# A graph layer on one core: the opening's transfers rearranged, and the one-hot of an edge step put back beside its selection

## The chip, the core and the metric

The kernel runs on one core of one Trainium2 chip. The metric is device time in microseconds (us), the median of three runs. The engines are named as the profile names them: PE (TensorE: matmuls; PEld is its weight loads), DVE (VectorE), ACT (ScalarE), POOL (GpSimd), SP (SyncE, which here only issues DMAs). "SPq", "ACTq" and so on are the engines' instruction queues, which issue DMAs.

## The reference

A graph has N = 12,500 nodes with 160 features each (64 scalars and 32 vectors of 3) and E = 400,000 edges, sorted by destination. What is computed, cut to what matters:

```python
h_s = s @ lin1_ws * a / sqrt(64)                   # s: 64 scalars of a node, a: its attribute
h_v = einsum('nci,cd->ndi', v, lin1_wv) * a / sqrt(32)
hid = silu(edge_scalars @ fc_w1 / sqrt(64))        # 64 scalars an edge
w1..w5 = split(hid @ fc_w2 / sqrt(64))             # 224 weights an edge
es, ev = h_s[edge_src], h_v[edge_src]              # gather
m_s = concat(w1*es*e0, w4 * sum_i(ev*e1) / sqrt(3))
m_v = concat((w2*es) x e1, w3*ev*e0, w5*cross(ev, e1) / sqrt(2))
agg = segment_sum(m, edge_dst) / sqrt(16)
pre = sc(s, v) * a + agg @ lin2 * a                # sc: another linear map of the node itself
x   = layernorm(x + gate(pre))                     # silu of 64 scalars, sigmoid gates of the vectors
```

## The kernel before

**Opening.** All nodes go through the first linear map. The nodes are taken 2048 at a time (`CH`), six full groups and one of 212. For each group SP's queue loads two halves of `xa` (64 scalars on partitions 0 to 63, two of the three vector components on 64 to 127, four DMAs of 64 x 1024 values) and `xz` (the third component, in four quarters of 512 nodes one under the other, four DMAs of 32 x 512), lines 269 to 281. PE multiplies by `l1` and by the block-diagonal `l1z`, DVE scales by the node's attribute into `ht`, and ACT's queue stores `ht` as rows of 640 B into the table `h_tab` in device memory (L345). Ahead of the node loads SP's queue issues three strided loads of `rows`, the first destination of each block of three tiles, 1042 values of 4 B taken one by one from `dst` (L254, L255). The function `bases` (L292) turns `rows` into a base for each block on all partitions (`lo`). After the node loads SP's queue loads the first edge indices and attributes (`index(0)`), the first chunk of edge scalars (`load_chunk(0)`), and the weights, `fc_w2` in ten pieces with its columns in another order. ACT's queue loads all destinations `dt` (L351) behind the stores of `h`; DVE subtracts the bases from them (`rel`, L387 and L392). The weights of the second map (`l2`) are loaded by SP (L380) and scaled by DVE one by one (L111). All this stands in an order written out by hand; the queues take it in that order, though the scaling of `l2` is mixed in with the first edge steps. DMAs of SP and ACT share eight completion semaphores in turn, and an issue waits for the DMA that had its semaphore before it.

**Edge steps.** 3125 tiles of 128 edges are taken four at a time: 782 steps. A step n

- gathers four tiles' rows of `h_tab` by the edges' sources: four indirect DMAs on POOL's queue into one of four buffers `hg` (L427);
- makes 224 weights an edge on PE (`pw`, L440) from `hid`, which PE (`ph`, L418) and ACT (L420) made two steps ahead for two steps at once, out of chunks of edge scalars `es` (L228) that SP loads;
- multiplies weights and rows on DVE, four instructions (`pr`, L450 once and L458 three times); the last of them frees the step's `hg` and `pw`;
- makes the selection on DVE: `one_hot` compares `rel` with 0 to 15 (`oh`, L503), and `select_quad` multiplies this by the four edge attributes (`sel`, L512);
- two steps later, multiplies `sel` and `pr` on PE into the sums of a pair of blocks (`pa`, L519).

Closed blocks are copied by ACT (L711), turned by PE (L528), mapped by `l2` sixteen at a time (`po`, L543) and added by DVE, block by block, to the accumulator `acc` at a position that depends on the data (L551, 1042 additions). Nodes whose blocks are done are finished four tiles at a time (L577 to L616) in between.

The order within a step is that of the program (`manual_schedule`). The loop before has the one-hot a step ahead and the additions at the first of the four products' gaps:

```python
oh = one_hot(edge, steps[0][2])
for n, (c, i, tiles) in enumerate(steps):
    ...
    pr = products(edge, pw, hg, len(tiles), [first, lambda: None])   # first: pops 1 or 2 additions
    sel = select_quad(edge, tiles, oh)
    for a in ready:
        add(*a)
    if n + 1 < len(steps):
        oh = one_hot(edge, steps[n + 1][2])
```

`first` pops two additions in even steps and one in odd ones; they are executed behind the selection.

Of the kernel before, what the change touches and what calls it, by code (L numbers as in the profile page):

```python
# [10 lines left out]
F32 = mybir.dt.float32  # L11
# [9 lines left out]
P = 128  # L21
S = 64
V = 32
# [5 lines left out]
BT = 3  # L29
# [3 lines left out]
KB = 4  # L33
SIDE = KB * BT
CT = 2 * SIDE
AHEAD = 3 * CT
# [4 lines left out]
NWT = 224  # L41
# [12 lines left out]
def gnn_kernel(  # L54
# [21 lines left out]
    nc = tc.nc  # L76
    N = x.shape[0]
    NT = attr.shape[1]
# [4 lines left out]
    NB = -(-TT // BT)  # L83
# [3 lines left out]
    consts = ctx.enter_context(tc.tile_pool(name="consts", bufs=1))  # L87
    dram = ctx.enter_context(tc.tile_pool(name="dram", bufs=1, space=bass.MemoryType.DRAM))
    h_tab = dram.tile([N, D], F32, name="h_tab")
# [5 lines left out]
    in_order = ctx.enter_context(ExitStack())  # L95
    in_order.enter_context(tc.manual_schedule(
        engines={ENG.PE, ENG.DVE, ENG.Activation, ENG.Pool, ENG.SP}))
    at = consts.tile([P, NT], F32, name="at")
    nc.scalar.dma_start(at, attr)

    l1 = consts.tile([P, P], F32, name="l1")
    nc.vector.memset(l1, 0.0)
    nc.scalar.dma_start(l1[:S, :S], lin1_ws)
    for i in range(2):
        r = slice(S + i * V, S + (i + 1) * V)
        nc.scalar.dma_start(l1[r, r], lin1_wv)
    scales = [(l1[:S], 1.0 / math.sqrt(S)), (l1[S:], 1.0 / math.sqrt(V))]

    def scale():
        for m, by in scales:  # L110
            nc.vector.tensor_scalar_mul(m, m, by)  # L111
        scales.clear()

    def block_diagonal(name, w, n, scale, queue=nc.scalar):
        k = w.shape[0]
        m = consts.tile([n * k, n * k], F32, name=name)
        nc.vector.memset(m, 0.0)
        for i in range(n):
            queue.dma_start(m[i * k:(i + 1) * k, i * k:(i + 1) * k], w)
        if scale != 1.0:  # L120
            scales.append((m, scale))
        return m

    l1z = block_diagonal("l1z", lin1_wv, 4, 1.0 / math.sqrt(V))
    for m, by in scales:
        nc.scalar.mul(m, m, by)
    scales.clear()


    rel = consts.tile([P, TT], I16, name="rel")  # L130
    rows = consts.tile([1, NB], I32, name="rows")
    early = consts.tile([1, 1], F32, name="early")
# [8 lines left out]
    ends_pool = ends.enter_context(tc.tile_pool(name="ends", bufs=1))  # L141
# [21 lines left out]
    steps = []  # L163
# [3 lines left out]
    slot_of = {}  # L167
# [23 lines left out]
    def index(t):  # L191
        a0, idx, _ = ahead(t)
        return idx[:, t - a0:t - a0 + 1]
# [20 lines left out]
    def in_pairs(a):  # L214

        return a.rearrange("o (c k h) -> o h c k", k=KB, h=2)

    ess = {}

    def load_chunk(c):  # L220
        if c in ess:
            return
        t0, halves = chunks[c]
        es = ess[c] = loads.tile([2 * S, SIDE * P], F32, name="es")
        for half, n in enumerate(halves):
            to = es[half * S:(half + 1) * S]
            e0 = (t0 + half * halves[0]) * P
            nc.sync.dma_start(to[:, :n * P], es_t[:, e0:e0 + n * P])  # L228


    ident = consts.tile([P, P], F32, name="ident")
# [9 lines left out]
    w2 = consts.tile([2 * S, 2, NWT], F32, name="w2")  # L241
# [4 lines left out]
    even = NB // (2 * KB) * 2 * KB  # L246
# [1 line left out]
                   base=0, channel_multiplier=0)  # L248
    nc.gpsimd.iota(share[:, even:], pattern=[[RATE, NB - even]], base=even * RATE, channel_multiplier=0)

    with nc.allow_non_contiguous_dma(reason="the first destination of each block"):
        firsts = dst[0:1, 0:(even - 1) * BT + 1:BT].rearrange("o (c h k) -> o h c k", k=KB, h=2)
        for half in range(2):
            nc.sync.dma_start(in_pairs(rows[:, :even])[:, half], firsts[:, half])  # L254
        nc.sync.dma_start(rows[:, even:], dst[0:1, even * BT:(NB - 1) * BT + 1:BT])  # L255


    U = 4
    dt = ends_pool.tile([P, TT], I32, name="dt")
    lo = ends_pool.tile([P, NB], F32, name="lo")  # L260
    CH = 4 * U * P
    starts = list(range(0, N, CH))
    with tc.tile_pool(name="nodes", bufs=len(starts)) as nodes, tc.tile_pool(
        name="nodes_ps", bufs=6, space=PSUM
    ) as nps, tc.tile_pool(name="z_ps", bufs=2, space=PSUM) as zps:
        loaded = []
        for c0 in starts:
            cn = min(CH, N - c0)
            quarters = 4 if cn == CH else 1
            assert quarters == 4 or cn <= U * P  # L270
            xa = nodes.tile([P, CH], F32, name="xa")
            for b0 in range(0, cn, CH // 2):
                b1 = min(b0 + CH // 2, cn)
                nc.sync.dma_start(xa[:S, b0:b1], xs_t[:, c0 + b0:c0 + b1])
                nc.sync.dma_start(xa[S:, b0:b1], xv_t[:2 * V, c0 + b0:c0 + b1])
            xz = nodes.tile([P, U * P], F32, name="xz")
            cq = cn // quarters
            for q in range(quarters):
                nc.sync.dma_start(xz[q * V:(q + 1) * V, :cq],
                                  xv_t[2 * V:, c0 + q * cq:c0 + (q + 1) * cq])  # L280
            loaded.append((c0, cn, quarters, cq, xa, xz))
        index(0)
        load_chunk(0)
        for half in range(2):
            r = slice(half * S, (half + 1) * S)
            nc.sync.dma_start(w1[r, r], fc_w1)
            at_c = 0
            for a, b in ((64, 128), (0, 64), (192, 224), (160, 192), (128, 160)):
                nc.sync.dma_start(w2[r, half, at_c:at_c + b - a], fc_w2[:, a:b])
                at_c += b - a  # L290

        def bases():  # L292

            base_f = ends_pool.tile([1, NB], F32, name="base_f")
            nc.vector.tensor_copy(base_f, rows)
            for b0 in range(0, NB, U * P):
                b1 = min(NB, b0 + U * P)
                ps = nps.tile([P, U, P], F32, name="hp").rearrange("p u c -> p (u c)")
                nc.tensor.matmul(ps[:, :b1 - b0], ones, base_f[:, b0:b1], start=True, stop=True)
                nc.scalar.copy(lo[:, b0:b1], ps[:, :b1 - b0])  # L300
            nc.vector.tensor_sub(share, rows, share)
            nc.vector.tensor_reduce(early, share, AX.X, OP.min)
            nc.vector.tensor_scalar(early, early, -float(MARGIN), None, op0=OP.is_lt)

        for c0, cn, quarters, cq, xa, xz in loaded:
# [4 lines left out]
            first = c0 // P  # L310
# [14 lines left out]
                                            at[:n, first + full:first + full + 1], None, op0=OP.mult)  # L325

            pz = zps.tile([P, U, 4, V], F32, name="pz")
            k = quarters * V
            for u in range(-(-cq // P)):
                n = min(P, cq - u * P)  # L330
                nc.tensor.matmul(pz[:n, u, :quarters].rearrange("p q c -> p (q c)"),
                                 xz[:k, u * P:u * P + n], l1z[:k, :k], start=True, stop=True)
            if quarters == 4:
                nc.vector.tensor_mul(
                    ht[:, :, P:].rearrange("p (q u) c -> p u q c", q=4), pz,
# [5 lines left out]
            if cn > full * P:  # L341
                n = cn - full * P
                nc.vector.tensor_scalar(ht[:n, full, P:], pz[:n, full, 0],
                                        at[:n, first + full:first + full + 1], None, op0=OP.mult)
            nc.scalar.dma_start(  # L345
                h_tab[c0:c0 + full * P, :].rearrange("(q p) d -> p q d", p=P), ht[:, :full])
            if cn > full * P:
                nc.scalar.dma_start(h_tab[c0 + full * P:c0 + cn, :], ht[:n, full])


    nc.scalar.dma_start(dt, dst)  # L351
    iota = consts.tile([P, W], F32, name="iota")
    nc.vector.tensor_copy(iota, iota_i)
    nc.vector.tensor_scalar_mul(w2, w2, 1.0 / math.sqrt(64))

    scs = consts.tile([S, V3], F32, name="scs")
    nc.sync.dma_start(scs, sc_ws)
# [137 lines left out]
            sorted_eat[a0] = eas  # L495
        return sorted_eat[a0]

    def one_hot(pool, tiles):

        n = len(tiles)  # L500
        t0 = slot_of[tiles[0][0]]
        oh = pool.tile([P, Q, W], F32, name="oh4")[:, :n]
        nc.vector.tensor_tensor(oh, rel[:, t0:t0 + n, None].to_broadcast([P, n, W]),  # L503
                                iota[:, None, :].to_broadcast([P, n, W]), op=OP.is_equal)
        return oh

    def select_quad(pool, tiles, oh):

        n = len(tiles)
        u = slot_of[tiles[0][0]] % AHEAD  # L510
        sel = pool.tile([P, Q, 4, W], F32, name="sel", bufs=3)
        nc.vector.tensor_mul(  # L512
            sel[:, :n], oh[:, :, None, :].to_broadcast([P, n, 4, W]),
            by_slot(tiles[0][0])[:, u:u + n, :, None].to_broadcast([P, n, 4, W]))
        return sel
# [112 lines left out]
    with tc.tile_pool(  # L628
# [132 lines left out]
        def add_up(n):  # L761

            if not adds or adds[0][0] > n:
                return []
            _, b, os, k, base = adds.pop(0)
            waiting.discard(blocks_of(b // 2)[b % 2])
            return [(base, os, k)]
# [15 lines left out]
        with tc.manual_schedule(engines={ENG.PE, ENG.DVE, ENG.Activation, ENG.Pool}):  # L783
# [3 lines left out]
            pieces = list(range(0, N, CHN))  # L787
            products_due = []
            checks = farthest(late)
            oh = one_hot(edge, steps[0][2])  # L790
            for n, (c, i, tiles) in enumerate(steps):
                if 2 <= n < 2 + ZP // 2:
                    for k in range(2):
# [11 lines left out]
                def first(n=n):  # L805
                    if rest:
                        rest()
                    for _ in range(2 - n % 2):
                        ready.extend(add_up(n))

                pr = products(edge, pw, hg, len(tiles), [first, lambda: None])
                sel = select_quad(edge, tiles, oh)
                for a in ready:
                    add(*a)
                if n + 1 < len(steps):
                    oh = one_hot(edge, steps[n + 1][2])
                if step_on:
                    step_on()
                begin()
# [153 lines left out]
```

## Time and profile before

| | |
|---|---|
| median of three runs | 5045.04 us (5044.53 to 5065.4) |
| profiled execution, time | 5044.53 us |
| profiled execution, span | 5042.8 us |
| first gather issued | 78.36 us |
| first product of the edge steps | 92.58 us |
| busy: PE, POOL, DVE, ACT | 78%, 59%, 47%, 18% |
| granted clock of PE, mean | 0.885 |
| mean rate of all DMAs | 82 GB/s |

A busy share is an average over the opening and 782 steps that are alike. Which wait ends last in a step is read from the idle time ahead of an engine's instruction and from what ended it. "remote" is a release that the profile can't put down to an instruction close by.

### The profile page before, as it was taken

Reading aid. Unit: us, or ns where it says so; the run is one execution under the profiler, and the core shown is the slowest. Engines: PE = TensorE matmul, PEld = TensorE weight load, DVE = VectorE, ACT = ScalarE, POOL = GpSimd, SP = SyncE. Lnnn points to the kernel's source line nnn. Section 1 sums busy time; section 2 is a strip of 40 time slices with the busy share of each in tenths; the row PEclk is TensorE's granted clock in tenths of the full one; section 3 lists DMA queues with packets and bytes.
Section 4 is the critical chain, followed back from the end, with each engine's and each line's share of the span. In section 5 each row is a group of like instructions: output and inputs, shape, how many; then the busy total and the mean of one; then the engine's idle time right before and its main releaser. Section 6 shows DMA issues by size and latency. Waiting matters only on the chain. (4 is left out here: it accounts for less than half of the span.)

```text
span 5042.8 us, 47689 instructions
## 1 busy us (share of the span) xinstructions
PE 3954.1 (78%) x14291; PEld 1696.2 (34%) x14291; DVE 2348.6 (47%) x6374; ACT 928.2 (18%) x2463; POOL 2991.5 (59%) x3134
## 2 busy tenths in 40 slices
PE   5777878778778888778878777778777877788877
PEld 3333333333333333333333333333333333333333
DVE  4444444444444544445444444444444544444444
ACT  1211121111111111112112111111111221211212
POOL 3565656665666666655666665656655665566563
PEclk8889988888989898888899888889888888888888
DMA  7333333333333333333333333333333333333332
GB/s 195 75 75 81 83 79 79 84 83 75 81 73 86 81 80 84 88 72 79 87 75 81 81 79 81 82 75 77 81 81 74 82 83 76 80 73 87 74 72 51
DMA packets 241211, 411.77 MB, mean 82 GB/s; under 512 B 74200, under 2 KB 171876, under 8 KB 240820
## 3 DMA queue, kind: packets, MB, share of 16 engines
q0 software_dynamic: 150000, 256.20, 21.5%
q1 hardware_dynamic: 77666, 142.75, 12.0%
q10 hardware_dynamic: 13282, 9.69, 0.7%
q8 instruction: 119, 1.95, 0.2%
q14 instruction: 144, 1.18, 0.1%
HBM read 392.40 MB, written 16.00 MB: 81 GB/s over the span
## 5 line engine op out<-in xcount | busy, mean ns | idle before, releaser
L427 POOL DMA_INDIRECT hg<-h_tab,idx x3125 | 2986.7, 956 | 2007.2 <-DVE pr L458 1035.3
L440 PE MATMUL pw<-w,hid 128*128 128x448 f32 x3126 | 1511.6, 610 | 292.5 <-ACT hid L420 103.3
L450 DVE TENSOR_TENSOR pr<-pw,hg 128x512 f32<-128x512 f32 x782 | 538.0, 688 | 2480.9 <-remote 1156.8
L519 PE MATMUL pa<-pr,sel 128*64 128x416 f32 x6250 | 1374.5, 556 | 57.9 <-issue 48.3
L458 DVE TENSOR_TENSOR pr<-pw,hg 128x384 f32<-128x384 f32 x2346 | 1152.3, 545 | 2.4 <-issue 2.2
L440 PEld LDWEIGHTS pw<-w,hid 128*128 128x128 f32 x3126 | 605.8, 212 | 821.9 <-issue 657.2
L519 PEld LDWEIGHTS pa<-pr,sel 128*64 128x64 f32 x6250 | 405.8, 144 | 964.2 <-issue 866.4
L528 PE MATMUL pt<-ident,sa 128*128 128x128 f32 x2084 | 360.6, 299 | 431.1 <-ACT hid L420 266.3
L711 ACT COPY sa<-pa 128x416 f32<-128x416 f32 x521 | 265.7, 510 | 1748.7 <-remote 626.5
L528 PEld LDWEIGHTS pt<-ident,sa 128*128 128x128 f32 x2084 | 258.5, 151 | 760.1 <-issue 368.3
L418 PE MATMUL ph<-es,w 128*128 128x512 f32 (+1 forms) x784 | 447.2, 653 | 42.3 <-ACT tt L533 13.1
L543 PE MATMUL po<-tt,l 128*96 128x256 f32 (+5 forms) x1496 | 376.0, 402 | 65.7 <-ACT tt L533 38.5
L420 ACT ACTIVATE hid<-ph 128x512 f32<-128x512 f32 x392 | 234.4, 598 | 968.5 <-remote 479.3
L512 DVE TENSOR_TENSOR sel<-oh,eas 128x256 f32<-128x256 f32 x782 | 324.4, 415 | 0.6 <-issue 0.5
L543 PEld LDWEIGHTS po<-tt,l 128*96 128x96 f32 (+1 forms) x1496 | 240.8, 173 | 223.1 <-issue 102.8
L531 ACT COPY tt<-pt 128x192 f32<-128x192 f32 x521 | 165.6, 318 | 772.4 <-remote 206.1
L418 PEld LDWEIGHTS ph<-es,w 128*128 128x128 f32 x784 | 118.4, 190 | 311.3 <-issue 258.5
L551 DVE TENSOR_TENSOR acc<-acc,os 96x32 f32 x1042 | 205.2, 197 | 18.9 <-ACT os L546 7.1
L503 DVE TENSOR_TENSOR oh<-rel,iota 128x64 f32<-128x64 int16 x782 | 170.0, 217 | 0.0
L533 ACT COPY tt<-pt 128x64 f32<-128x64 f32 x521 | 117.2, 225 | 0.0
L420 ACT ACT_TABLE_LOAD x48 | 61.6, 1283 | 248.4 <-remote 187.9
L546 ACT COPY os<-po 96x512 f32<-96x512 f32 (+2 forms) x68 | 38.3, 563 | 312.2 <-PE po L543 118.6
(77 smaller groups left out, 614.9 us busy)
## 6 DMA issues: line engine op xcount, KB each, us to landing
es<-in_es_t_dram SPq DMA_DIRECT2D x260, 384.0 KB
hg<-h_tab,idx POOLq DMA_INDIRECT x3125
h_tab<-ht ACTq DMA_DIRECT2D x6, 1280.0 KB
xt<-in_x_dram SPq DMA_DIRECT2D x23, 320.0 KB
out_dram<-y SPq DMA_DIRECT2D x23, 320.0 KB
xv<-in_xv_t_dram SPq DMA_DIRECT2D x25, 187.5 KB
xs<-in_xs_t_dram SPq DMA_DIRECT2D x25, 125.0 KB
xa<-in_xs_t_dram SPq DMA_DIRECT2D x12, 256.0 KB
```

Source lines behind the costliest of these rows:

```text
L418: nc.tensor.matmul(ph[:k, c], w1[:k, :k], es[:k, t0 * P + c0 * P:t0 * P + c1 * P], start=True, stop=True)
L420: nc.scalar.activation(hid[:k, c], ph[:k, c], AF.Silu, scale=1.0 / math.sqrt(64))
L427: nc.gpsimd.indirect_dma_start(out=hg[:, t, :], out_offset=None, in_=h_tab, in_offset=bass.IndirectOffsetOnAxis(ap=i, axis=0))
L440: nc.tensor.matmul(pw[:, t:t + m, :NWT], hid[:m * S, c * P:(c + 1) * P], w2[:m * S, :m], start=True, stop=True)
L450: nc.vector.tensor_mul(two, pw[:, :n, :2 * S].rearrange("p t (k c) -> p t k c", k=2), hg[:, :n, None, :S].to_broadcast([P, n, 2, S]))
L458: nc.vector.tensor_mul(pr[:, :n, first:first + V3].rearrange("p t (i c) -> p t i c", i=3), pw[:, :n, None, 2 * S + k * V:2 * S + (k + 1) * ...
L512: nc.vector.tensor_mul(sel[:, :n], oh[:, :, None, :].to_broadcast([P, n, 4, W]), by_slot(tiles[0][0])[:, u:u + n, :, None].to_broadcast([P ...
L519: nc.tensor.matmul(pa[half * ROWS:(half + 1) * ROWS, :NPR], sel[:, t].rearrange("p k w -> p (k w)"), pr, start=start, stop=stop)
L528: nc.tensor.transpose(pt[:, four * P:four * P + k], sa[:k, c:c + P], ident[:k, :k])
L543: nc.tensor.matmul(po[:, k, :nb], l2[r, terms[to, part, four]], a[:, :nb], start=(n == 0), stop=(n == len(of) - 1))
L551: nc.vector.tensor_add(window, window, os[:, :, b])
L711: nc.scalar.copy(sa, pas.pop(j)[:, :NPR])
```

## The change

- The loads of a node group are three DMAs instead of eight: 64 x 2048, 64 x 2048, and for `xz` one DMA of 128 rows, which now stand with the quarter as the fast index of the partition; `l1z` is laid out to match.
- The first group's loads are the first of SP's queue; the weights of the first map (ACT's queue) and the other groups follow.
- The strided loads of `rows` are gone. One row of `dst` (3125 values) is loaded to partition 0 on ACT's queue, and DVE copies the bases out of it at the start of `bases`, in three instructions.
- The stores of `h` (the full rows of tiles), the first chunk of edge scalars and all of `dt` go on POOL's queue, ahead of the gathers. The last 84 rows are stored on SP's queue.
- `fc_w2` is loaded in one piece for each half, and DVE orders and scales it in ten instructions instead of one.
- In a step, the one-hot is made just ahead of its selection, in `select_quad`; the additions are popped one in each of two gaps, so up to two in every step.

In the built program the scalings of `l2` now all stand ahead of the first product on DVE, and SP's loads of `l2` behind the store of the last 84 rows.

```diff
-    with nc.allow_non_contiguous_dma(reason="the first destination of each block"):
-        firsts = dst[0:1, 0:(even - 1) * BT + 1:BT].rearrange("o (c h k) -> o h c k", k=KB, h=2)
-        for half in range(2):
-            nc.sync.dma_start(in_pairs(rows[:, :even])[:, half], firsts[:, half])
-        nc.sync.dma_start(rows[:, even:], dst[0:1, even * BT:(NB - 1) * BT + 1:BT])
...
+        def load(c0):
...
-            for b0 in range(0, cn, CH // 2):
-                b1 = min(b0 + CH // 2, cn)
-                nc.sync.dma_start(xa[:S, b0:b1], xs_t[:, c0 + b0:c0 + b1])
-                nc.sync.dma_start(xa[S:, b0:b1], xv_t[:2 * V, c0 + b0:c0 + b1])
+            nc.sync.dma_start(xa[:S, :cn], xs_t[:, c0:c0 + cn])
+            nc.sync.dma_start(xa[S:, :cn], xv_t[:2 * V, c0:c0 + cn])
             xz = nodes.tile([P, U * P], F32, name="xz")
             cq = cn // quarters
-            for q in range(quarters):
-                nc.sync.dma_start(xz[q * V:(q + 1) * V, :cq],
-                                  xv_t[2 * V:, c0 + q * cq:c0 + (q + 1) * cq])
+            z = xv_t[2 * V:, c0:c0 + cq]
+            if quarters == 4:
+                nc.sync.dma_start(xz[:, :cq], bass.AP(tensor=z.tensor, offset=z.offset,
+                                                      ap=[[z.ap[0][0], V], [cq, 4], [1, cq]]))
+            else:
+                nc.sync.dma_start(xz[S:S + V, :cq], z)
             loaded.append((c0, cn, quarters, cq, xa, xz))
+
+        load(starts[0])
...
+        nc.scalar.dma_start(dt[0:1], dst[0:1])
+        for c0 in starts[1:]:
+            load(c0)
         index(0)
-        load_chunk(0)
+        raw = ends_pool.tile([2 * S, NWT], F32, name="raw")
...
         def bases():
 
+            firsts = dt[0:1, 0:(even - 1) * BT + 1:BT].rearrange("o (c h k) -> o h c k", k=KB, h=2)
+            for half in range(2):
+                nc.vector.tensor_copy(in_pairs(rows[:, :even])[:, half], firsts[:, half])
+            nc.vector.tensor_copy(rows[:, even:], dt[0:1, even * BT:(NB - 1) * BT + 1:BT])
...
-            nc.scalar.dma_start(
+            nc.gpsimd.dma_start(
                 h_tab[c0:c0 + full * P, :].rearrange("(q p) d -> p q d", p=P), ht[:, :full])
             if cn > full * P:
-                nc.scalar.dma_start(h_tab[c0 + full * P:c0 + cn, :], ht[:n, full])
-
-
-    nc.scalar.dma_start(dt, dst)
+                nc.sync.dma_start(h_tab[c0 + full * P:c0 + cn, :], ht[:n, full])
+
+
+    load_chunk(0, nc.gpsimd)
+    nc.gpsimd.dma_start(dt, dst)
...
-    def one_hot(pool, tiles):
+    def select_quad(pool, tiles):
...
-                    for _ in range(2 - n % 2):
-                        ready.extend(add_up(n))
-
-                pr = products(edge, pw, hg, len(tiles), [first, lambda: None])
-                sel = select_quad(edge, tiles, oh)
+                    ready.extend(add_up(n))
+
+                pr = products(edge, pw, hg, len(tiles), [first, lambda n=n: ready.extend(add_up(n))])
+                sel = select_quad(edge, tiles)
                 for a in ready:
                     add(*a)
-                if n + 1 < len(steps):
-                    oh = one_hot(edge, steps[n + 1][2])
```

## The prediction

> **What bounds the kernel now.** I read the page's costliest groups first, then the list of waits, and then the timeline of the opening and of a piece in the middle. The groups show who is busy and who waits.
>
> ```profile
> span 5042.8 us, 47689 instructions
> ...
> L427 POOL DMA_INDIRECT hg<-h_tab,idx x3125 | 2986.7, 956 | 2007.2 <-DVE pr L458 1035.3
> ...
> L450 DVE TENSOR_TENSOR pr<-pw,hg 128x512 f32<-128x512 f32 x782 | 538.0, 688 | 2480.9 <-remote 1156.8
> ...
> L458 DVE TENSOR_TENSOR pr<-pw,hg 128x384 f32<-128x384 f32 x2346 | 1152.3, 545 | 2.4 <-issue 2.2
> ...
> L512 DVE TENSOR_TENSOR sel<-oh,eas 128x256 f32<-128x256 f32 x782 | 324.4, 415 | 0.6 <-issue 0.5
> ...
> L503 DVE TENSOR_TENSOR oh<-rel,iota 128x64 f32<-128x64 int16 x782 | 170.0, 217 | 0.0
> ```
>
> GpSimd issues 3125 gathers. From the first at 78.36 us to the end of the last (4998.3 + 0.95) are 4920.9 us, and these are 2986.7 us of issue and 2007.2 - 73.0 us of idle time. VectorE waits 2480.9 us, nearly always ahead of the first product of a step (L450). The waits say for what GpSimd's idle time is:
>
> ```profile
> POOL hg L427 <- DVE pr L458: 1035.3, 262, 10.8
> POOL hg L427 <- issue: 947.6, 2798, 73.0
> ```
>
> 0.30 us between two gathers is the queue's own; 1035.3 us in 262 waits go to the last product of a step, which frees one of four `hg` buffers. Such a wait looks like this in the timeline:
>
> ```profile
> 2523.89 0.69 DVE L450 TENSOR_TENSOR pr<-pw,hg 128x512 f32<-128x512 f32 x1 [10.34 <-remote]
> ...
> 2525.89 0.41 DVE L512 TENSOR_TENSOR sel<-oh,eas 128x256 f32<-128x256 f32 x1
> ...
> 2526.24 0.94 POOL L427 DMA_INDIRECT hg<-h_tab,idx  x1 [5.26 <-DVE pr L458]
> 2526.39 0.21 DVE L503 TENSOR_TENSOR oh<-rel,iota 128x64 f32<-128x64 int16 x1
> ```
>
> VectorE had been idle for 10.34 us; four products then run end to end, and GpSimd goes on 2.35 us after the first of them began. So the time is the opening up to the gathers, plus gathers, plus waits that end with a product's end. The selection (L512), the one-hot (L503) and the additions (L551) stand behind the products.
>
> The opening is the second thing that the change touches:
>
> ```profile
> 0.75 1.99 SPq L254 DMA_DIRECT2D rows<-in_dst_dram  x2
> ...
> 7.22 0.54 SPq L274 DMA_DIRECT2D xa<-in_xs_t_dram  x1
> ...
> 74.93 0.80 ACTq L351 DMA_DIRECT2D dt<-in_dst_dram  x1
> ...
> 78.36 1.13 POOL L427 DMA_INDIRECT hg<-h_tab,idx  x1 [73.00 <-issue]
> ...
> 85.67 6.26 DVE L387 TENSOR_TENSOR rel<-dt,lo 128x260 int16<-128x260 int32 x12
> ...
> 108.05 0.94 POOL L427 DMA_INDIRECT hg<-h_tab,idx  x1 [3.81 <-DVE l L111]
> ```
>
> The strided loads of `rows` hold SP's queue until 7.22 us. Then the DMA engines are the bound:
>
> ```profile
> 20.00:30.00 10.00, 5.78 (x52) 5.58 (x51) 5.09 (x8) 0.00 (x0) 0.00 (x0) 0.90 1.05 290
> ...
> 50.00:60.00 10.00, 6.73 (x59) 6.38 (x57) 5.61 (x9) 0.00 (x0) 0.00 (x0) 1.00 1.07 294
> ...
> 90.00:100.00 10.00, 4.08 (x8) 1.75 (x8) 6.64 (x25) 3.49 (x3) 7.56 (x9) 0.81 0.31 70
> ```
>
> The last three columns are clock, DMA share and GB/s: the 16 engines are full (1.05, 1.07) until `dt` has landed, and not after.
>
> **The opening, worked out.** By the packet records, full 2048-node groups take 1536 packets of 4096 B at 265 ns and 768 of 2048 B at 138 ns: (407 + 106) / 16 = 32.1 us. The stores of h are 12,500 rows of 640 B at 36 ns: 28.1 us. `dt` is 128 x 590 ns / 16 = 4.7 us, the first edge scalars 128 x 419 ns / 16 = 3.4 us. Sum 68.3 us of full engines; between the first node load's issue (7.22) and the subtraction that waits for `dt` (85.67) lie 78.4 us, so 10.1 us are latency and gaps.
>
> In the changed kernel the first node load stands first on SP, where L254 began at 0.75 us. The strided loads are gone; the bases come from one 12.5 KB row on ScalarE's queue and three small copies on one partition of VectorE. The nearest row, the conversion of 1042 values (L295), is 0.68 us, so at most 2 us in all, amid nodes work that waits for DMA: nothing, or 2 us if VectorE were the bound there. With the same 78.4 us `dt` lands at 79.2 (6.5 us earlier). If the gaps shrink, because loads no longer share eight completion semaphores with the stores (SP waited 23.0 us in 3 waits for `h_tab<-ht`), down to 2 us, it is 71. I take 75, the middle: 10.7 us earlier.
>
> Two things follow. First, the weights of the second linear map: before, VectorE scaled each as it came, between the first products (L111, up to 107.69 + 0.36), and the 21st gather waited for that until 108.05. Their loads wait on SP behind 27 issues of about 0.65 us, 18 us, which in the new order begin when the last node group is done, some 20 us before `dt`; so the scalings, now all ahead of the first product, are bare time: 21 x 0.18 = 3.8 us. First product at 75 + 6.7 (L387 and L392) + 3.8 = 85.5, instead of 92.58. Ten scalings of the raw weights replace one of 0.40 us: at 0.2 us each 2 us, ahead of the wait for `dt`, hidden. Second, the gathers: they need the stores landed, 8.1 us (`dt`, scalars) before `dt`, so from about 67 on; sixteen take 16 x 1.25 = 20 us to 87, the first buffer is free at 85.5 + 2.2 = 87.7, and the 17th starts at 88, not 99.45; the 21st at 93, not 108.05. Gains of 11.5 and 15; I take 13 us. What is late next is PE's weights, in the usual rhythm.
>
> **The edge steps.** A step's VectorE work is the same 2.16 us of products, 0.41, 0.21 and the additions. Before, the one-hot of step n stood ahead of its product, now behind. Where VectorE was idle before a product, the product starts as soon as PE lets it, in both. In a burst of m steps after that, the chain to the last product is m products and m-1 times the rest, in both. So the gathers' releases do not move: 0. The selection ends up to 0.21 us later, and PE reads it two steps on (12 us): hidden; without that cover, 782 x 0.21 = 164 us, but in the list of waits PE's weight loads wait for `sel` 13.3 us in all, 12 times. Additions go 2 a step for 8 of 12 steps instead of 1.5 for 11; the 1042 x 0.197 us stay. A step with two in place of one makes the next product up to 0.2 us later if VectorE is the late one; bounds from below and above are 0.2 us for a third of the 262 waits, -17 and +17 us. I take 0.
>
> The profiled execution took 5044.53 us, 1.7 us around its span, 0.5 us under the median of 5045.04. Sum: 5044.5 - 13 + 0 = 5031.5; I say 5032.
>
> **The price that no row shows: stores on GpSimd's queue.** Each of the six stores has 2048 rows. The nearest row is a gather of 128 rows, 0.95 us; ScalarE's queue needed 0.37 us for a store. If the 0.95 us is all fixed, six stores are 6 us, hidden between node groups. If it is all per row, a store is 16 x 0.95 = 15.1 us. I take a third of that, 5 us, since GpSimd is idle until 78 us: 15 + 6 x 5 = 45 us, ahead of the stores' own data, so nothing on the path. Below 8.3 us each it stays hidden (15 + 6 x 8.3 = 65).
>
> The Trainium skill, "DMA: Bandwidth & Descriptors", section "Issuing engines are not separate DMA queues", says that DMAs started on several engines run on the same 16 and that this saves only the issuing time. This is the rule against the change: by it the stores gain nothing from moving, and the opening would keep its 68.3 us and gain only the 6.5 us at the front, 5038. The same page's "Latency and other measured facts" puts the software path's first byte at about 1 us; no row here shows a store on it, and by that figure an estimate is 6 us for six stores, hidden.
>
> **Rivals.** *Stores bound by GpSimd (slower).* The first group was ready 13 us after its load's issue (7.22 to 20.29), so now at about 15. At 15.1 us each the last store is issued at 106; about 3 us for the small store, the scalars and `dt`, and 8.1 us of their data put `dt` at 117, the first product at 127.5, the 21st gather at 135 to 137 against 108: +28, 5072. With a price g it comes at 15 + 6g + 3 + 25 = 43 + 6g, so from g = 10.8 us a store on the kernel is slower than before. For: 0.95 us for 128 rows. Against: a gather also reads its indices. Chance 0.18; further 0.05 for a rhythm that loses over 25 us through later selections.
>
> *Opening and rhythm both better (faster).* Gaps go to 2 us (15 to 17 us in all) and the even additions save up to 17 us of the waits: 5044.5 - 16 - 12 = 5016. For: 262 waits, each ended by VectorE. Against: nearly all of them begin with an idle VectorE. Chance 0.25.
>
> *The change saves only the front.* The engines stay full and the gaps stay 10.1 us: 5044.5 - 6.5 = 5038. Chance 0.12. The forecast has 0.40.
>
> **Numbers.** 0.5% is 25 us, about what a measurement of this kernel can tell from no change. Forecast and front alone fall within it: same 0.52; faster 0.25; slower 0.23. The range goes from the faster case's deeper half (5010) to the GpSimd case's price (5072); the likeliest case's own is 5020 to 5043.
>
> **What would show it.** Right: first node load issued near 1 us, `dt`'s subtraction near 75, first product near 85, 21st gather near 93, and GpSimd's wait for products still about 1035 us. Wrong: stores of over 8 us each on GpSimd's queue; a wait sum that moved by over 25 us, which would say that the selection's place or the additions set the releases; PE waiting for `sel`.

## The result, and the profile after

The changed kernel took 5024.9 us (median of 20 runs, 4984.79 to 5047.46), the kernel before beside it 5051.62 us (20 runs, 5035.62 to 5078.56). The ratio is 0.9939, with a 95% interval of 0.9918 to 0.9959: 0.61% faster, 31 us of the mean of the runs; the medians are 26.7 us apart. The forecast was 5032, in a range from 5010 to 5072. The time lies in the range and in the forecast's own, 5020 to 5043, but on the other side of the 0.5% bound, where 0.25 of the chance had been put; the interval reaches across that bound. As a change, 13 us had been forecast, and about 31 (21 to 41) were measured. The profiled execution took 5013.31 us. Single runs of one kernel lie mostly 10 to 20 us, and up to 40, to either side of their median, so one pair of profiles can't show a term of 13 us in the total. What repeats from profile to profile is what to go by: times in the opening, durations, counts.

The costliest groups of the changed kernel, with busy time, mean of one in ns, idle time before them and its main releaser, as in the prediction:

```profile
span 5011.5 us, 47586 instructions
...
L438 POOL DMA_INDIRECT hg<-h_tab,idx x3125 | 3014.2, 965 | 1897.3 <-DVE oh L515 955.2
...
L461 DVE TENSOR_TENSOR pr<-pw,hg 128x512 f32<-128x512 f32 x782 | 539.1, 689 | 2323.0 <-remote 1189.2
...
L518 DVE TENSOR_TENSOR sel<-oh,eas 128x256 f32<-128x256 f32 x782 | 338.0, 432 | 44.0 <-DVE oh L515 1.4
```

Two things have moved that the prediction held still. The gathers' own time is up from 2986.7 to 3014.2 us, and the waits for a buffer are down from 1035.3 to 955.2. They now carry the name of the one-hot (L515) because it follows the last product at once; it is still the product that frees the buffer: in both profiles a gather that waited begins 0.27 us after the last product's end. The selection (L518) takes 432 ns on average, not 415.

The timeline of the opening; columns are start, time, engine, line, and in brackets the idle time before with what ended it:

```profile
0.76 0.58 SPq L235 DMA_DIRECT2D xa<-in_xs_t_dram  x1
1.39 0.58 SPq L236 DMA_DIRECT2D xa<-in_xv_t_dram  x1
8.45 0.60 SPq L241 DMA_DIRECT2D xz<-in_xv_t_dram  x1
...
17.84 1.39 POOL L350 DMA_DIRECT2D h_tab<-ht  x1 [12.47 <-DVE ht L339]
...
51.20 1.15 POOL L350 DMA_DIRECT2D h_tab<-ht  x1 [3.31 <-DVE ht L339]
...
65.03 1.04 POOL L438 DMA_INDIRECT hg<-h_tab,idx  x1 [9.60 <-DMA h_tab<-ht]
...
68.58 6.36 DVE L398 TENSOR_TENSOR rel<-dt,lo 128x260 int16<-128x260 int32 x12 [14.14 <-DMA dt<-in_dst_dram]
...
75.31 4.18 DVE L261 TENSOR_SCALAR l<-l 32x96 f32<-32x96 f32 x20
...
79.63 0.68 DVE L461 TENSOR_TENSOR pr<-pw,hg 128x512 f32<-128x512 f32 x1
...
92.38 0.94 POOL L438 DMA_INDIRECT hg<-h_tab,idx  x1 [0.30 <-issue]
...
113.42 0.94 POOL L438 DMA_INDIRECT hg<-h_tab,idx  x1 [6.36 <-DVE oh L515]
```

A store takes GpSimd 1.15 to 1.39 us. The first gather waits for the last store to land, and the first wait for a buffer comes only at 113.42: until then no gather waits for `dt` or for the scalings (L261). The first seven gathers, 65.03 to 73.40, take 8.9 us instead of 6.6, beside the subtraction (L398) for the most part. In the windows, clock, DMA share and GB/s are the last three columns:

```profile
30.00:40.00 10.00, 8.78 (x37) 6.69 (x38) 5.45 (x8) 1.25 (x3) 0.38 (x1) 0.66 1.03 364
...
50.00:60.00 10.00, 1.10 (x10) 0.83 (x8) 2.74 (x18) 0.00 (x0) 3.35 (x5) 0.76 1.04 350
```

The engines are as full as before (1.03 and 1.04), but they move 364 and 350 GB/s, not 294 at best.

**Where the 31 us went.** The spans of the two profiles differ by 31.3 us. I take the span apart into what lies outside the gathers, the gathers' own time, the 0.305 us that the queue takes between two (3124 x 0.305 = 952.8) and all idle time beyond that. Before: 121.9 + 2986.7 + 952.8 + 981.4 = 5042.8. After: 109.6 + 3014.2 + 952.8 + 934.9 = 5011.5. So -12.3 for the opening and the tail, +27.5 for gathers that got longer, -46.5 for waits. The forecast had -13 and 0.

### The profile page after: what moved, and what is told of

Same layout as the page of the kernel before. It is cut to its first block, busy times and chain, and to the rows that moved or that the text cites. A ratio compares the mean times of both kernels' runs of the same rounds, so it can differ in the third digit from the quotient of the medians.

```text
span 5011.5 us, 47586 instructions
## 1 busy us (share of the span) xinstructions
PE 3956.4 (79%) x14291; PEld 1685.8 (34%) x14291; DVE 2436.2 (49%) x6386; ACT 926.2 (18%) x2463; POOL 3028.5 (60%) x3144
## 5 line engine op out<-in xcount | busy, mean ns | idle before, releaser
L438 POOL DMA_INDIRECT hg<-h_tab,idx x3125 | 3014.2, 965 | 1897.3 <-DVE oh L515 955.2
L525 PE MATMUL pa<-pr,sel 128*64 128x416 f32 x6250 | 1398.3, 559 | 82.2 <-issue 67.1
L549 PE MATMUL po<-tt,l 128*96 128x256 f32 (+5 forms) x1496 | 358.7, 389 | 41.1 <-ACT tt L539 26.3
L518 DVE TENSOR_TENSOR sel<-oh,eas 128x256 f32<-128x256 f32 x782 | 338.0, 432 | 44.0 <-DVE oh L515 1.4
L557 DVE TENSOR_TENSOR acc<-acc,os 96x32 f32 x1042 | 194.7, 187 | 26.0 <-ACT os L552 6.9
L515 DVE TENSOR_TENSOR oh<-rel,iota 128x64 f32<-128x64 int16 x782 | 169.2, 216 | 0.0
L583 PE MATMUL pp<-ident,acc 96*128 96x96 f32 x196 | 38.1, 281 | 127.0 <-DVE acc L557 57.6
```

Source lines behind the costliest of these rows:

```text
L438: nc.gpsimd.indirect_dma_start(out=hg[:, t, :], out_offset=None, in_=h_tab, in_offset=bass.IndirectOffsetOnAxis(ap=i, axis=0))
L518: nc.vector.tensor_mul(sel[:, :n], oh[:, :, None, :].to_broadcast([P, n, 4, W]), by_slot(tiles[0][0])[:, u:u + n, :, None].to_broadcast([P ...
L525: nc.tensor.matmul(pa[half * ROWS:(half + 1) * ROWS, :NPR], sel[:, t].rearrange("p k w -> p (k w)"), pr, start=start, stop=stop)
L549: nc.tensor.matmul(po[:, k, :nb], l2[r, terms[to, part, four]], a[:, :nb], start=(n == 0), stop=(n == len(of) - 1))
L557: nc.vector.tensor_add(window, window, os[:, :, b])
```

## The experiments

Theory A is the prediction's: the opening gives all, the step order nothing. Rival B: the step order gives the other half. The runs were made on three chips (for the first pair of profiles the chip is not on record), four kernels on each beside the kernel before: its medians are 5107.4 us (first four), 5047.79 (second four) and 4068.19 (last four). Ratios are to the kernel before on the same chip.

| run | opening | one-hot | additions | first gather at | gathers' own time | waits beyond the pace | ratio, interval |
|---|---|---|---|---|---|---|---|
| before, first profile | before | step's end | 2 and 1 | 78.36 | 2986.7 | 981.4 | 1 |
| changed, first profile | changed | at selection | 1 + 1 | 65.03 | 3014.2 | 934.9 | 0.9939, 0.9918 to 0.9959 |
| e1_open | changed | step's end | 2 and 1 | 69.20 | 2991.0 | 1022.6 | 0.9992, 0.9971 to 1.0013 |
| e2_step | before | at selection | 1 + 1 | 77.40 | 3017.7 | 999.2 | 1.002, 0.9996 to 1.0044 |
| e5_again | changed | at selection | 1 + 1 | 68.93 | 3008.2 | 951.5 | 0.9958, 0.9938 to 0.9978 |
| e6_open_again | changed | step's end | 2 and 1 | 69.65 | 2983.9 | 1022.5 | 1.0004, 0.9973 to 1.0034 |
| e9_adds | changed | step's end | 1 + 1 | 69.53 | 2986.8 | 0 | 0.9929, 0.9916 to 0.9943 |
| e10_oh | changed | at selection | 2 and 1 | 67.17 | 3013.4 | 0 | 0.998, 0.997 to 0.9991 |
| e11_step_again | before | at selection | 1 + 1 | 77.73 | 3018.4 | 0 | 1.003, 1.0018 to 1.0041 |

**e1_open: the opening alone.** The loop has the step order of before.

```diff
-                    ready.extend(add_up(n))
-                pr = products(edge, pw, hg, len(tiles), [first, lambda n=n: ready.extend(add_up(n))])
-                sel = select_quad(edge, tiles)
+                    for _ in range(2 - n % 2):
+                        ready.extend(add_up(n))
+                pr = products(edge, pw, hg, len(tiles), [first, lambda: None])
+                sel = select_quad(edge, tiles, oh)
...
+                if n + 1 < len(steps):
+                    oh = one_hot(edge, steps[n + 1][2])
```

> The changed opening with the edge steps of before (one-hot at a step's end, additions two and one). In the profiled pair the 21st gather came 15.7 us earlier (92.38 against 108.05), while the profiled time fell by 31 us. Theory A (the step order is worth 0, as predicted, and the rest of the 31 us is spread from run to run): first gather near 65, 21st gather near 92, ratio to before 0.997 (-13 to -16 us of 5050), GpSimd's wait for the products about 1035 us within the spread. Rival B (the step order gives the other 15 us): the same opening, and the same 0.997; it differs from A in the run with the step order alone. Rival C (the opening gives all): 0.994 here.

The opening is there (first gather 69.20, 21st 95.41), the gain in the total is not: 0.9992. The interval just reaches the 0.997 of theory A; rival C is out.

**e2_step: the step order alone.** The kernel before with the other lines of that diff.

> The opening of before with the edge steps of the changed kernel (one-hot just ahead of its selection, additions one in each of two gaps). Theory A (step order worth 0): first gather at 78, 21st at 108, ratio 1.000 within +-0.003. Rival B (fewer or shorter waits for products): ratio 0.997 or less, GpSimd's wait for products some 15 to 80 us under 1035. Rival C (opening gives all): 1.000.

1.002. Rival B's 0.997 is outside the interval. The gathers took 3017.7 us as in the changed kernel, so their 27 us (26.7 here, against e1_open on the same chip) come from the step order and not from the opening.

**e3_act: stores back on ScalarE's queue.**

```diff
-            nc.gpsimd.dma_start(
+            nc.scalar.dma_start(
                 h_tab[c0:c0 + full * P, :].rearrange("(q p) d -> p q d", p=P), ht[:, :full])
             if cn > full * P:
-                nc.sync.dma_start(h_tab[c0 + full * P:c0 + cn, :], ht[:n, full])
+                nc.scalar.dma_start(h_tab[c0 + full * P:c0 + cn, :], ht[:n, full])
```

> The changed kernel with the stores of h issued by ScalarE's queue again; first edge scalars and all destinations stay on GpSimd's queue, loads and steps as changed. Theory Q (the queue decides how a store is cut: 4480-byte packets at 205.6 ns on GpSimd's queue, 640-byte packets at 35.7 ns on ScalarE's): 12,500 packets of 640 B again, 27.9 us of 16 engines in place of 22.8, first gather about 5 us later than 65 (70), and ratio to before about 0.995. Rival (the queue is indifferent; the stores ran faster because the loads' packets were longer or the loads were done): packets and time of the stores as in the changed kernel, first gather 65. Second rival (a store on ScalarE's queue shares completion semaphores with the loads, so gaps come back too): first gather 72 or later.

By the packet records the stores are 12,500 packets of 640 B at 35.6 ns again, 27.8 us of 16 engines, in place of 4480-byte packets at 205.6 ns, 22.8 us: theory Q holds, the queue decides how a store is cut. The first gather came at 75.24, not 70. The timeline of GpSimd has one reason, and the waits of SP's queue have another (in their lines: us in total, times, longest):

```profile
5.33 1.30 POOL L196 DMA_DIRECT2D es<-in_es_t_dram  x2
29.76 0.56 POOL L357 DMA_DIRECT2D dt<-in_dst_dram  x1 [23.13 <-DVE rows L297]
75.24 1.45 POOL L438 DMA_INDIRECT hg<-h_tab,idx  x1 [44.92 <-DMA l<-in_lin_ws_dram]
```

```profile
SPq L241 <- DMA h_tab<-ht: 11.3, 1, 11.3
SPq L235 <- DMA h_tab<-ht: 11.1, 1, 11.1
```

With no stores ahead of them on GpSimd's queue, scalars and `dt` are issued at 5.33 and 29.76, and their 7.3 us of the engines (3.4 + 3.9) go ahead of all stores (scalars) or of the last four (`dt`). And two issues of node loads wait 22.4 us for stores to land, which no node load does in the changed kernel; that is the second rival, with its first gather at 72 or later. So the stores' packets are one gain of the move, and their place and the loads' freedom from them are others; how the 10.2 us divide is not shown. Ratio 0.9978 (0.9952 to 1.0003).

**e4_loads: the loads of a group in two halves again.**

```diff
-            nc.sync.dma_start(xa[:S, :cn], xs_t[:, c0:c0 + cn])
-            nc.sync.dma_start(xa[S:, :cn], xv_t[:2 * V, c0:c0 + cn])
+            for b0 in range(0, cn, CH // 2):
+                b1 = min(b0 + CH // 2, cn)
+                nc.sync.dma_start(xa[:S, b0:b1], xs_t[:, c0 + b0:c0 + b1])
+                nc.sync.dma_start(xa[S:, b0:b1], xv_t[:2 * V, c0 + b0:c0 + b1])
```

> The changed kernel with the 64-row loads of a node group cut in two halves again (64 x 1024 values, 4096 bytes a packet); the third component stays one load, stores, destinations and steps as changed. Theory P (a longer packet has a higher rate: 8192 B at 494.5 ns is 16.6 GB/s an engine against 15.5 of 4096 B at 264.9): loads cost 25.4 us of 16 engines in place of 23.7, first gather 1.7 us later (66.7); 12 more issues on SP of 0.6 us are hidden. Rival (issues and shared completion semaphores make gaps): first gather 68 or later, SP waiting on the queue. Rival (nothing): 65. The time itself moves by less than 0.1% in the first and last case: 0.994 of before, as the changed kernel.

All three were wrong: the first gather came at 60.38, earlier than in any other profile (63.5 to 69.7 with the changed opening otherwise). 4096-byte packets took 232.6 ns here, 17.6 GB/s an engine, against 16.6 for 8192 bytes in the changed kernel; it is not the packet's size that made the loads faster than before (264.9 ns for the same size there). What did is not shown. Ratio 0.9974 (0.9946 to 1.0002).

**e5_again and e6_open_again: the whole change and the opening alone, on one chip.**

> The changed kernel once more, unaltered, beside the opening alone. Theory A (step order worth 0, opening worth 13 to 16 us): ratio to before 0.997, the same as the opening alone. Rival B (opening and step order together give more than either alone, or the 0.9939 of the first comparison holds everywhere): 0.994, and 0.003 or more under the opening alone. First gather at 65 to 69, 21st at 92 to 96 in both cases.

> The opening alone, as in the first such run, unaltered, to be set beside the changed kernel on the same chip. Theory A: 0.997 like the changed kernel, first gather 65 to 69. Rival B: 0.997 to 0.999, with the changed kernel 0.003 or more below it.

0.9958 and 1.0004. Half of rival B is right: the step order is worth some 0.4% here on top of the new opening, though by itself, on the first chip, it gave nothing (e2_step). On that chip the changed kernel itself did not run; its two nearest relatives (e3_act, e4_loads) are not clear of e1_open there. By the table this is the first pair again: gathers +24 us, waits -71 in the profiles. The profiled e6_open_again was 24 us above its median, so about -50 is nearer for the waits.

**e7_sel_twice: a dose on VectorE.** The selection's multiplication is done twice in the changed kernel.

```diff
+        for _ in range(2):
-        nc.vector.tensor_mul(
+            nc.vector.tensor_mul(
```

> The changed kernel with the selection's multiplication done twice in every step: 782 x 0.432 us = 338 us more on VectorE behind the products. A dose on the rest of a step, far above the 0.2 us that the moved one-hot and additions shift. Theory A, in the working of the prediction (only a step whose products follow the step before without idle time passes the delay on): 506 of 782 steps begin behind over 0.3 us of idle VectorE, so at most 276 x 0.43 = 119 us, ratio to the changed kernel 1.00 to 1.024, and a shift of 0.2 us in some steps is worth under 50 us and may well be 0. Rival (VectorE's whole step sets the releases): 338 us, ratio 1.067. Rival (another engine sets them, VectorE's rest is covered): under 25 us, ratio under 1.005.

The page has 1564 selections, and the time did not move: 0.9955 (0.993 to 0.9981) beside 0.9958.

```profile
L519 DVE TENSOR_TENSOR sel<-oh,eas 128x256 f32<-128x256 f32 x1564 | 671.2, 429 | 70.4 <-issue 0.5
```

333 us more on VectorE cost nothing that shows: what stands behind the products is covered, so 0.2 us here or there in it does not delay the releases. The prediction's reason for its 0 holds as far as it goes.

**e8_pe_less: a dose on PE.** For the middle tile of each block the kernel leaves out half of the columns of the sums.

```diff
+        c = NPR if start or stop else NPR // 2
-        nc.tensor.matmul(pa[half * ROWS:(half + 1) * ROWS, :NPR],
-                         sel[:, t].rearrange("p k w -> p (k w)"), pr, start=start, stop=stop)
+        nc.tensor.matmul(pa[half * ROWS:(half + 1) * ROWS, :c],
+                         sel[:, t].rearrange("p k w -> p (k w)"), pr[:, :c], start=start, stop=stop)
```

> The changed kernel with the sums of the middle tile of each block taken over 208 columns of 416: it leaves out half of the sums of one tile in three, and spares PE about 2083 x 0.28 us = 583 us of 3956 busy. What bounds the edge steps? Theory G (GpSimd's issue plus waits for products that PE's pace sets): the 955 us of waits shrink by most of what PE is spared, time down by 300 to 580 us, ratio 0.88 to 0.94. Rival (gathers and their own queue time bound the steps; PE has slack): under 50 us, ratio over 0.99.

0.9951 (0.993 to 0.9972): nothing. The dose was smaller than I had written, since two of these matmuls run side by side: the group fell from 1392.7 us in e5_again to 1200.0, PE as a whole by 147. GpSimd's wait for products stayed:

```profile
L438 POOL DMA_INDIRECT hg<-h_tab,idx x3125 | 3022.2, 967 | 1910.5 <-DVE oh L515 969.7
...
L526 PE MATMUL pa<-pr,sel 128*64 128x416 f32 (+1 forms) x6250 | 1200.0, 498 | 89.5 <-issue 66.7
```

PE's granted clock fell from 0.884 to 0.867 on the way, so part of what was spared may have gone to a lower clock. With doses of 333 us on VectorE and 147 us on PE, neither engine's amount of work is seen to set the waits on this chip; what a larger dose on PE would do was not tried.

**e9_adds and e10_oh: the step order split.** e9_adds is e1_open with the additions one in each gap; e10_oh is the changed kernel with two and one.

> The changed opening, the additions one in each of two gaps as changed, but the one-hot at a step's end as before. So far the opening alone gave 0.9992 and 1.0004 of before, the whole change 0.9939 and 0.9958. Theory O (the one-hot's place behind the products gives the missing 0.4%): here 1.000, GpSimd's waits of over 2 us about 218 times as with the old order, gathers of over 1.1 us about 60. Theory D (the even additions give it): here 0.995, about 203 waits. Prediction's view (neither matters): no difference to the opening alone nor to the whole change, which the first four comparisons speak against.

> The changed opening, the one-hot just ahead of its selection as changed, but the additions two and one as before. Theory O (the one-hot's place gives the 0.4%): here 0.995, waits of over 2 us about 203 times, gathers of over 1.1 us about 235. Theory D (the even additions): here 1.000, about 218 waits.

The third chip gave PE a clock of 0.96 instead of 0.88, and in no profile there does GpSimd wait for products. e9_adds, its groups:

```profile
span 4040.3 us, 47595 instructions
...
L438 POOL DMA_INDIRECT hg<-h_tab,idx x3125 | 2986.8, 956 | 966.5 <-issue 851.7
```

No gap between two of the 3125 gathers is over 0.45 us. The time is the opening, 3125 gathers at the queue's pace, and the tail; runs of one kernel agree within 0.3%, and small terms can be read. e9_adds against e10_oh differ by 2986.8 and 3013.4 us of gathers: with the one-hot at the step's end they are 26.6 us shorter. The medians are 4041.6 and 4061.1, 0.5% apart. The order of the two ratios is theory D's, but not its mechanism: there are no waits to save, and e12_deep (below), with the additions of e9_adds, the one-hot of e10_oh and a fifth buffer, has gathers of 3014.1 us and a median of 4066.6. So it is neither O nor D: where no waits are left, the one-hot's new place costs its 27 us of gathers, and in the medians 19.5 to 25 us.

**e11_step_again: the step order alone on that chip.**

> The step order alone (opening of before) once more; it gave 1.002 [0.9996, 1.0044]. Theory I (opening and step order only give something together): 1.000 to 1.002 again. Theory S (the step order is worth 0.3 to 0.5% wherever it stands, and the first comparison was off): 0.995 to 0.998. 21st gather at 107 to 108 either way.

1.003 (1.0018 to 1.0041): slower, as the longer gathers say, though by 12.6 us and not by 27. The kernel before was not profiled on this chip, so the difference stays open.

**e12_deep: five buffers.**

```diff
-        name="deep", bufs=4
+        name="deep", bufs=5
```

> The changed kernel with five buffers of gathered rows instead of four. GpSimd waits about 970 us for the product that frees the oldest buffer. Theory G (the wait is for buffers; gathers could run further ahead): the first wait comes after 20 gathers, waits fall by 200 us or more, ratio to before under 0.96. Rival (the pace is set elsewhere, and the buffers fill up once whatever their number): waits about 970 us as before, ratio 0.993 to 0.997, as the changed kernel.

On a chip without waits this can't tell its two theories apart, and says nothing of the waits elsewhere. But where no gather waits, a fifth buffer changes nothing, so it stands for the changed kernel there: 0.9994 (0.9985 to 1.0003), no gain.

```profile
span 4065.6 us, 47574 instructions
...
L438 POOL DMA_INDIRECT hg<-h_tab,idx x3125 | 3014.1, 965 | 961.7 <-issue 852.9
```

The span of e9_adds is 25.3 us under it: first gather 4.4 later, gathers 27.3 shorter, 2.4 less after the last gather. It is the fastest kernel on that chip (0.9929). On the other two only its near relative ran, the opening alone (e1_open, e6_open_again), with no gain, so it is not shown to be better everywhere.

The same run also prices the opening in the total: e11_step_again has the same steps behind the opening of before, and its median is 14.2 us higher (4080.79 against 4066.56; the runs of either lie within 9 us).

**Which gathers get longer.** From the records I sorted the gathers by what VectorE had begun last, and was still executing, at the moment when the gather began; "long" is over 1.0 us, against a usual 0.946.

| VectorE as the gather begins | before: gathers, long | changed: gathers, long | e9_adds | e10_oh |
|---|---|---|---|---|
| nothing | 1600, 1 | 1518, 1 | 1379, 0 | 1369, 1 |
| a product | 824, 0 | 873, 0 | 1084, 0 | 1079, 1 |
| selection, begun 0.06 us ago or more, 0.2 us or more left | 40, 40 | 251, 251 | 51, 51 | 224, 224 |
| selection, under 0.2 us left | 89, 54 | 36, 3 | 182, 7 | 51, 8 |
| selection, begun under 0.06 us ago | 47, 14 | 106, 11 | 44, 16 | 105, 39 |
| one-hot | 124, 21 | 109, 1 | 119, 17 | 90, 3 |
| addition | 306, 12 | 128, 0 | 161, 10 | 100, 2 |
| something else | 95, 20 | 104, 30 | 105, 22 | 107, 16 |

Products do not slow a gather (1 long of 3860 in these four). In either order it is mostly the selection that does: every gather that begins with 0.2 us or more of a selection left is long, and it ends 0.81 to 0.84 us after that selection's end. So it is held from about 0.13 us after its beginning until the selection is done. What the new order changed is how often a gather begins there, 251 times instead of 40.

The reason stands in the timelines. A gather that waited for a buffer begins 0.27 us after the last product's end, in every profile with such waits. In the kernel before, the selection follows that product at once and is nearly over by then (2525.89 + 0.41 against 2526.24 in the lines of the prediction): 0 of 288 such gathers are long. In the changed kernel the one-hot comes between, and the selection has just begun:

```profile
1047.82 0.21 DVE L515 TENSOR_TENSOR oh<-rel,iota 128x64 f32<-128x64 int16 x1
1048.07 0.42 DVE L518 TENSOR_TENSOR sel<-oh,eas 128x256 f32<-128x256 f32 x1
1048.17 1.14 POOL L438 DMA_INDIRECT hg<-h_tab,idx  x1 [5.33 <-DVE oh L515]
...
113.39 0.49 DVE L518 TENSOR_TENSOR sel<-oh,eas 128x256 f32<-128x256 f32 x1
113.42 0.94 POOL L438 DMA_INDIRECT hg<-h_tab,idx  x1 [6.36 <-DVE oh L515]
```

Of the 252 gathers that waited, 169 begin 0.10 us after the selection did and take 0.19 us more, 32.8 us together. Another 76 begin 0.03 us after it: they are not held, but the selection takes 490 ns instead of 425. Gathers that did not wait give 5.7 us back, and the difference is the 27 us. On the third chip no gather waits, and yet 224 of e10_oh's begin in such a selection against 51 of e9_adds'; what sets their moment there was not followed. All ten profiles with the new place lie between 3008.2 and 3029.7 us, all four with the old one between 2983.9 and 2991.0.

The Trainium skill, "SBUF — State Buffer", section "SBUF: two separate sides", says that VectorE and GpSimd share one pair of ports, that an operation of VectorE with two inputs in SBUF can hold it for the whole instruction against a GpSimd operation that reads SBUF, and that a GpSimd DMA's descriptors need it. This case agrees: the products read `pw` from PSUM, have one input in SBUF, and slow a gather in none of 824 and 873 cases; a selection has two, and holds the gather to its end in 40 of 40 and 251 of 251. That it is these ports, and not something else that the two instructions share, no run here shows.

## Why the prediction was right or wrong

- **Opening, 13 us: right in its times, in part by luck.** First gather 65.03 (forecast 67), `dt`'s subtraction 68.58 (75), first product 79.63 (85.5), 17th gather 87.39 (88), 21st 92.38 (93). The gains are 13.3, 12.1 and 15.7 us at the 1st, 17th and 21st gather. With the same opening in other runs the first gather is at 63 to 70, a gain of 9 to 15. The first gather is near its forecast because two errors stood against each other: `dt` landed 6.4 us earlier than forecast, and the stores landed 3.6 us ahead of it, not 8.1. In the total the opening alone shows no gain on the first two chips (0.9992, 1.0004); on the third it is worth 14.2 us.
- **The 68.3 us of full engines: mis-sized.** They became 59.6: node loads 29.2 (forecast 32.1), stores 22.8 (28.1), `dt` 4.6, scalars 3.0. I kept the old packets' times for new packets. Against that, SP's third load was not issued until 8.45, so part of the 6.5 us at the front did not come. Nor were the engines full all the time in the kernel before: the windows 40 to 50 and 60 to 70 have shares of 0.76 and 0.84, so the prediction's "until `dt` has landed" holds for the windows that it shows.
- **The Trainium skill's rule against the change** ("DMA: Bandwidth & Descriptors", section "Issuing engines are not separate DMA queues") gave 5038. e3_act disagrees with it for this case: the queue also decided the packets, 640 or 4480 B, worth 5.0 us of 27.8.
- **A store on GpSimd, 5 us: mis-sized.** 1.15 to 1.39 us for 2048 rows, near the end where the gather's 0.95 us for 128 rows is all fixed. The slower rival needed 10.8 us and is out (its two figures do not agree: 43 + 6g is 134 at 15.1 us, and 135 to 137 stands beside it).
- **Scalings of `l2`, 3.8 us bare:** 4.18 us and ahead of the first product, as said. But the product was not what the 17th gather waited for, so they cost nothing.
- **Edge steps, 0: the step that failed.** "So the gathers' releases do not move: 0" followed VectorE's chain alone, and that part stands: the release stays 0.27 us behind the last product's end, and more work behind it costs nothing (e7_sel_twice). It left out that VectorE's instructions act on a gather while it is issued. At the release there had been the end of a selection, and now there was its beginning: +24 to +27 us on all three chips. And the waits did move: -46.5 us in the first pair, -71 in the second (about -50 by the medians). The prediction named a wait sum off by over 25 us as the sign of an error, and it was off by 80. That the time came out 7 us from 5032 is luck in part: these two terms stand against each other, and the kernel before had a median of 5051.62 beside it, not 5045.04.
- **The faster rival** (5016) had the right sign for the waits, by its even additions. Its mechanism is not shown: e9_adds and e10_oh ran where no waits are left.
- **Left open:** why the waits fall with opening and step order together (0.9939, 0.9958) and not with either alone (0.9992 and 1.0004; 1.002). The two lone ratios do not add up to the whole, and the place where the parts meet was not found. One thing goes with it: on the second chip the runs of e5_again had a mean granted clock of 0.8862 and those of e6_open_again 0.8814, and among the runs of e6_open_again alone the longer ones have the lower clock (correlation -0.71, about 51 us per 0.01). Whether the clock lengthens the waits or follows them is not shown.

## What to carry to other kernels

When instructions of one engine are reordered, look also at what another engine does beside them: sort its instructions by what the first engine was executing as each began, and compare their durations. Sorting by everything that overlapped a gather blurs this: in the kernel before, a one-hot also falls into 142 of the 162 long gathers, but mostly later than the selection that holds them. A move that is free on its own engine's chain can lengthen a neighbour's 3125 instructions by 27 us. And a gain that lives in a wait is worth only what the chip at hand waits: count the waits there before trusting it.

## What the runs showed of the hardware that I had not expected

- The same kernel took 5107, 5048 and 4068 us on three chips. On the first two, and in the first pair, PE's granted clock was 0.87 to 0.89 and GpSimd waited 935 to 1030 us beyond its pace in every profile; on the third it was 0.96, and no profile has such a wait (the kernel before was not profiled on these three). The two go together; that the clock makes the waits is not shown, and with less work on PE (e8_pe_less) the clock fell and the waits stayed.
- A gather that begins 0.10 us into a selection takes 0.19 us more; one that begins 0.03 us into it takes its usual time, and the selection 490 ns instead of 425. Whichever of the two came first held the other.
- A store of 2048 rows of 640 B was cut into packets of 4480 B on GpSimd's queue (21.8 GB/s an engine) and of 640 B on ScalarE's (18.0).
- A gather of 128 rows takes GpSimd's queue 1.25 us, 0.946 and 0.305, on every chip: 3125 of them are the floor of this kernel, 3.9 ms of its time, and the third chip runs on it.
